# Cross-attention on one core: GpSimd's written order, the last batch's stages, transposes for the attention

## The chip, the core and the metric

The kernel runs on one core of one Trainium2 chip. The core has five instruction queues that matter here: TensorE (PE in the profile; PEld is its weight loads), VectorE (DVE), ScalarE (ACT), GpSimd (POOL) and SyncE (SP, which issues the transfers). Each queue is worked off in its own order; semaphores order the queues among each other. The metric is the device time of one execution in microseconds (us). The kernel before took 420.76 us (median of 3 runs, 420.61 to 422.99).

## What is computed

Cross-attention over 8 batches, 112 queries, 371 text tokens and 4 prompt tokens, 20 heads of 16 channels. Cut to what matters:

```python
q   = heads(x @ W_q)                                   # B 8, S 112, C 320, H 20, Dh 16
k_t, v_t = heads(text @ W_k), heads(text @ W_v)        # text: first 371 of 375 tokens, E 512
probs_t  = softmax(q k_t * Dh**-0.5)
text_out = probs_t @ v_t
k_ip, v_ip = heads(ip @ W_k_ip), heads(ip @ W_v_ip)    # ip: the last 4 tokens
qsem  = l2norm(probs_t @ text)                         # per head: 112 x 512
fused = q k_ip * Dh**-0.5 + 0.5 * qsem @ l2norm(ip).T
probs_ip = softmax(fused) * spatial_mask[:, None]
out = (text_out + probs_ip @ v_ip) @ W_out + b_out + x
```

All of it is in float32. The kernel never forms qsem: the norm of probs @ text is the root of p G p, where G is the Gram matrix of the text tokens, so the kernel multiplies the probabilities with a matrix u that holds G (its lower blocks only, doubled off the diagonal), the products with the normalised prompts, a column of ones and the values.

## The kernel before

**Tiling.** Each batch has 5 groups of 4 heads. For a group, `scores` writes four score products (112 x 375) to PSUM banks, `probabilities` takes the negated row maximum on VectorE (line 757), the exponential on ScalarE (line 760) and a copy of the four prompt logits, `ipl` (line 762); `sent` stores the probabilities to the ring `xg` by a transfer, and `turned` transposes them in blocks on VectorE (line 778). `multiplied` (line 797) is the large product: 12 steps of four products in four row strips of TensorE, each step 32 tokens narrower than the last (392 to 40 columns), into four banks `ps_qd`. Each bank then holds p G for its head, and in its last 21 columns the four prompt products, the sum z and the 16 value sums. `value_sums` copies these 21 to `pvs` on ScalarE (line 810); `reduced` multiplies p G with p and sums on VectorE (line 843), into `ss`. In the last batch, and for two heads of the group before it, `shared` does that sum by a copy on ScalarE (line 828), a product on GpSimd (line 832) and a sum on ScalarE (line 836). `placed` puts the group's values into u on GpSimd (line 703).

**Beside it, one batch ahead,** run the keys (line 582), values (616), queries (381) and the Gram matrix (540) of the next batches, cut into pieces and spread over the groups by `between`.

**The end of a batch** is `finish`, a generator whose pieces are called from the loop by `run(("f", b), ...)`: z2 and the maximum rn = max(ss, z2) (lines 884 and 886), a root on ScalarE (901) between two table loads (Sqrt, then Exp), the division of the value sums by z on GpSimd (`divided`, 892), the fused prompt logits fu (908 to 914), their Exp (918), and the weights w (926). For batches 0 to 5 `prompt_sums_and_projection` weighs the prompt values on GpSimd (986 to 994), transposes the attention (`ps_a`, 999) and projects it (`ps_o`, 1011). For the last two batches the prompt values come by a product: w is transposed (`ps_wT`, 932), then attention and prompts are summed in one bank `ps_a` (946: a product with the identity; 949: a product with the prompt values `bd`). `bd` holds the prompt values of both batches by head; a memset (683) and two selects on GpSimd (686, in `own_channels`) clear what belongs to other heads. The last batch's first 16 heads go through `finish` (generator `first`), its last 4 through `last_heads` (`last`), with `projected_prompts` (`late`) multiplying their prompt values with W_out beforehand.

**What sets the order.** The kernel asks the framework to keep the written order on TensorE, SyncE and VectorE (and from the main loop on ScalarE). GpSimd's queue is ordered by the framework's scheduler until the last batch, and as written from there. So before the last batch a scheduler decides which of GpSimd's ready instructions comes first; afterwards the text does.

**Banks.** PSUM has three pools: four banks `qd`, two `sc` and two `mm` (`bank(name)` takes `mm`, `bank(name, spare=True)` takes `sc`). A product that gets a bank again waits until the last reader of its former tile is done. In the last batch the odd groups use `mm` and `sc` for `ps_qd`, and the scores of group five lie in `qd`.

**The last batch's loop** runs over its five groups g = 0 to 4 with the scores of group four made in group one (two at step 0, two at step 3) and those of group five in group two (steps 2 and 3). `sums` is the open generator of `shared`; `before` is the open `finish` of the seventh batch (b = 6), whose root stands between group one and two; `last_keys` and a piece of the queries lie there too.

## Time and profile before

| | |
|---|---|
| median of 3 runs (lowest to highest) | 420.76 us (420.61 to 422.99) |
| the profiled execution | 420.08 us |
| its span | 418.3 us |
| busy: TensorE, weight loads | 410.9 us, 321.4 us |
| busy: VectorE, ScalarE, GpSimd | 334.5 us, 216.3 us, 123.6 us |
| the large product, line 797 | 3840 records, 218.5 us |
| block transposes of the probabilities, line 778 | 79, 126.0 us |
| chain that ended last | TensorE 90%, VectorE 3%, GpSimd 2%, ScalarE 2%, transfers 2% |

The span is the time from the first to the last instruction or transfer of the profiled execution. A row of a timeline gives start, duration, engine, source line, operation, the tile written and the tiles read, a count and, in brackets, how long the engine stood idle before it and what ended that. Times of weight loads overlap those of products. A product in plain float32 shows as two records, a transpose as one.

### The profile page before, as it was taken

The numbers are of one execution on the slowest core, as the hardware profiler recorded it, in microseconds if no ns is written. First come the engines' busy times: TensorE is split into PE (matmuls) and PEld (weight loads), VectorE is DVE, ScalarE is ACT, GpSimd is POOL, SyncE is SP. The second block draws the span as 40 slices with busy tenths as digits, with TensorE's granted clock in tenths as the row PEclk, the third lists the DMA queues.
The fourth block names the chain that finished last, engine by engine and source line by source line (L and its number), as shares of the span: only waits on it lengthen the run. The fifth ranks groups of instructions, "written<-read, shape, count | busy, mean of one in ns | idle before, by whom it ended". The sixth has DMA issues, their size and how long they took to land.

```text
span 418.3 us, 14151 instructions
## 1 busy us (share of the span) xinstructions
PE 410.9 (98%) x5512; PEld 321.4 (77%) x5512; DVE 334.5 (80%) x724; ACT 216.3 (52%) x732; POOL 123.6 (30%) x308
## 2 busy tenths in 40 slices
PE   8999999999999999999999999999999999989996
PEld 8767777787778877788777877788678887677983
DVE  4037689988899889898898978899798977878774
ACT  2344334736365453746356353654538463765774
POOL 3611121112071114422062121712144120724540
PEclk9999999999999999999999999999999999999999
DMA  8777856557764455465554555554445355526201
GB/s 247 211 189 201 184 144 155 150 133 172 176 164 130 134 142 142 113 157 164 142 134 126 170 133 136 133 126 143 121 123 137 97 169 151 144 75 168 69 2 31
DMA packets 47578, 58.98 MB, mean 141 GB/s; under 512 B 10648, under 2 KB 41536, under 8 KB 47510
## 3 DMA queue, kind: packets, MB, share of 16 engines
q1 hardware_dynamic: 46878, 57.10, 51.8%
q10 hardware_dynamic: 632, 0.96, 0.8%
q8 instruction: 44, 0.72, 0.8%
q14 instruction: 24, 0.20, 0.2%
HBM read 16.79 MB, written 1.88 MB: 45 GB/s over the span
## 4 chain that ended last, share of the span: by engine, by line
PE 90%; DVE 3%; POOL 2%; ACT 2%; DMA 2%; issue 1%; SPq 0%; DVEq 0%; POOLq 0%
PE ps_qd L797 37%; PE ps_v L616 13%; PE ps_s L734 10%; PE ps_k L582 10%; PE ps_g L540 7%; PE ps_q L381 3%; PE ps_o L1011 3%; PE ps_g L496 1%; DMA xg<-p 1%; DVE nmx L757 1%; ACT p L760 1%; DVE xgT L778 1%; PE ps_w L472 1%; PE ps_o L966 1%; PE ps_k L598 1%; POOL wv L986 1%
## 5 line engine op out<-in xcount | busy, mean ns | idle before, releaser
L797 PE MATMUL ps_qd<-u,xgT 32*112 32x168 f32 (+11 forms) x3840 | 218.5, 351 | 0.0
L797 PEld LDWEIGHTS ps_qd<-u,xgT 32*112 32x112 f32 x3840 | 185.0, 172 | 27.2 <-issue 0.7
L778 DVE STREAM_TRANSPOSE xgT<-xg 128x512 f32<-128x512 f32 (+2 forms) x79 | 126.0, 1604 | 4.3 <-DMA xg<-p 3.9
L760 ACT ACTIVATE p<-ps_s,nmx 112x371 f32<-112x371 f32 x156 | 84.5, 579 | 86.5 <-DVE nmx L757 81.2
L757 DVE TENSOR_REDUCE nmx<-ps_s 112x1 f32<-112x371 f32 x160 | 78.4, 534 | 25.1 <-PE ps_s L734 24.1
L843 DVE CUSTOM_DVE_ANT_0 junk<-ps_qd,p 112x371 f32<-112x371 f32 x146 | 79.2, 543 | 20.3 <-ACT pvs L810 3.3
L703 POOL COPY u<-vr 128x64 f32<-128x64 f32 x120 | 26.7, 240 | 138.4 <-PE ps_qd L797 106.5
L734 PE MATMUL ps_s<-kT,qm 32*112 32x375 f32 (+1 forms) x320 | 65.8, 496 | 0.0
L616 PE MATMUL ps_v<-wv_sb,ctxT 128*128 128x384 f32 (+1 forms) x192 | 63.0, 477 | 0.0
L616 PEld LDWEIGHTS ps_v<-wv_sb,ctxT 128*128 128x128 f32 x192 | 35.7, 190 | 20.9
L582 PE MATMUL ps_k<-ctxT,wk_sb 128*128 128x371 f32 x136 | 46.9, 488 | 0.2 <-DVE ctxT L463 0.2
L734 PEld LDWEIGHTS ps_s<-kT,qm 32*112 32x112 f32 x320 | 25.6, 171 | 12.7 <-issue 10.8
L582 PEld LDWEIGHTS ps_k<-ctxT,wk_sb 128*128 128x128 f32 x136 | 24.4, 189 | 14.0 <-issue 0.5
L651 ACT COPY vr<-vext 32x240 f32<-32x240 f32 x84 | 32.7, 389 | 1.3
L623 ACT COPY vext<-ps_v 128x384 f32<-128x384 f32 (+1 forms) x24 | 11.2, 466 | 42.2 <-PE ps_v L616 42.2
L540 PE MATMUL ps_g<-ctxT 128*32 128x375 f32 (+11 forms) x672 | 30.4, 333 | 0.0
L540 PEld LDWEIGHTS ps_g<-ctxT 128*32 128x32 f32 x672 | 27.7, 110 | 2.0
L390 DVE TENSOR_SCALAR qm<-ps_q,emask 128x224 f32<-128x224 f32 (+1 forms) x25 | 9.0, 394 | 18.1 <-PE ps_q L381 18.0
L762 ACT COPY ipl<-ps_s 112x4 f32<-112x4 f32 x140 | 23.0, 165 | 0.0
L986 POOL TENSOR_TENSOR wv<-vip,w 112x1280 f32<-112x1280 f32 x6 | 14.8, 2468 | 22.2 <-DVE w L926 22.2
L512 ACT ACTIVATE ug<-ps_g 128x375 f32<-128x375 f32 (+2 forms) x24 | 8.3, 375 | 24.7 <-PE ps_g L540 12.5
L442 DVE STREAM_TRANSPOSE ctxT<-ct 128x512 f32<-128x512 f32 x18 | 20.0, 1113 | 0.0
(177 smaller groups left out, 344.2 us busy)
## 6 DMA issues: line engine op xcount, KB each, us to landing
xg<-p SPq DMA_DIRECT2D x156, 162.3 KB
u<-ug SPq DMA_DIRECT2D x124, 99.0 KB
ct<-in_ctx_dram SPq DMA_DIRECT2D x24, 176.0 KB
vip<-vipd SPq DMA_DIRECT2D x6, 560.0 KB
out_dram<-ob SPq DMA_DIRECT2D x8, 140.0 KB
ct<-in_ctx_dram SPq DMA_DIRECT2D x4, 256.0 KB
x_sb<-in_x_dram SPq DMA_DIRECT2D x7, 140.0 KB
xr_sb<-in_x_dram SPq DMA_DIRECT2D x28, 35.0 KB
```

The lines of the kernel that those rows point to most:

```text
L540: nc.tensor.matmul(ps[c][q * RG : (q + 1) * RG, j * RG - c * P : T - c * P], ctxT[:, e, j * RG : (j + 1) * RG], ctxT[:, e, j * RG : T], st ...
L582: nc.tensor.matmul(ps[:, :TT], wk_sb[:, e, i * P : (i + 1) * P], s["ctxT"][:, e, :TT], start=(e == 0), stop=(e == NE - 1),)
L616: nc.tensor.matmul(ps[:, :w], ctxT[:, e, c * P : (c + 1) * P], wv_sb[:, e, :w], start=(e == 0), stop=(e == NE - 1),)
L651: copy(s["vr"][a * RG : (a + 1) * RG, q::QN].rearrange("p c g d -> p c (g d)"), s["vext"][q * RG : (q + 1) * RG, :, a * w : (a + 1) * w],)
L703: nc.gpsimd.tensor_copy(v, dealt(b, c, s["vr"][:, c * QN : (c + 1) * QN, g, :]))
L734: nc.tensor.matmul(ps[:S, :w], qm[a * RG : (a + 1) * RG, i, r, j * S : (j + 1) * S], s["kT"][a * RG : (a + 1) * RG, i, :w], start=True, st ...
L757: nc.vector.tensor_reduce(nmx, ps[:S, :TT], AX.X, ALU.max, negate=True)
L760: nc.scalar.activation(s["p", g][:, a, :], ps[:S, :TT], AF.Exp, bias=nmx)
L762: nc.scalar.copy(s["ipl"][:, groups[g][a], :], ps[:S, TT:T])
L778: nc.vector.transpose(xT[:, j0:j1].rearrange("p j (k q) -> p q j k", q=QN), xg[:, :, j0 * RG : j1 * RG].rearrange("p q (j k) -> p q j k", ...
L797: nc.tensor.matmul(banks[a][:S, j * RG : UW], xT[a * RG : (a + 1) * RG, j, :S], region(b, c)[a * RG : (a + 1) * RG, q, j * RG - c * P :], ...
L843: nc.vector.tensor_tensor_reduce(out=junk, in0=ps[:S, :TT], in1=s["p", g][:, a, :], scale=1.0, scalar=0.0, op0=ALU.mult, op1=ALU.add, accu ...
```

## The change

1. From the seventh batch's third group on (three steps before the last batch, at `n == len(steps) - NG - 3`) GpSimd too runs in written order, instead of from the last batch on. Its queue changes: in the fifth group of that batch the prompt sums of batch six (986 to 994) come ahead of the copies of vr, and the selects on bd behind these and the next copies into u.
2. The prompt logits of the first batch (`prompt_logits`) move behind the pieces that `between` issues: on TensorE behind the key transposes and a query product, on ScalarE behind the copy of kT.
3. `probabilities` is split into `maxima` and `exponentials`. In the last batch, `finish` of the seventh starts ahead of the loop (z2, reciprocal, division, then the bias and a table load for Sqrt); its maximum, root and the load of Exp come in step 0 of group one, between the maxima and the exponentials of the two held heads. The ScalarE sums of `shared` are drained at step 0 of group one, at the start of group two, and at step 8 of groups three and four. fu comes at step 4 of group two, behind the maxima for group five, its Exp at step 8, w at step 8 of group three.
4. The tail: `value_sums` of the last group come behind the copy of wT and in the order 0, 3, 2, 1; the third value copy of group four comes ahead of the last sum; the Sqrt table is loaded earlier; `last_heads` takes reciprocal and quotient ahead of the last reduction, and its transpose later; the copies `bw` and of the last `aT` move from ScalarE to VectorE; the last batch's `ps_a` takes an `sc` bank.
5. The identity products of `ps_a` in the last two batches become transposes (`is_transpose=True`), and the warming product `warm` ahead of them goes.

```diff
-    def warm(ps, n):
-        for _ in range(n):
-            nc.tensor.matmul(ps[:, NC * P :], ident, ident, start=True, stop=True)
...
+    def maxima(b, g, a):
+        s = st[b]
+        nmx = small.tile([S, 1], F32, tag="nmx", name=f"nmx_{b}_{g}_{a}", bufs=4)
+        nc.vector.tensor_reduce(nmx, s["sc", g, a][:S, :TT], AX.X, ALU.max, negate=True)
+        s["mx", g, a] = nmx
...
     def probabilities(b, g, a, hold=False):
-        s = st[b]
-        ps = s.pop(("sc", g, a))
-        nmx = small.tile([S, 1], F32, tag="nmx", name=f"nmx_{b}_{g}_{a}", bufs=4)
-        nc.vector.tensor_reduce(nmx, ps[:S, :TT], AX.X, ALU.max, negate=True)
+        maxima(b, g, a)
+        exponentials(b, g, a)
+        if not hold:
+            sent(b, g, a)
...
 finish:
+        def divided():
+            nc.vector.reciprocal(zr, z)
+            eng.tensor_tensor(
+                ah, pvs[:, :, NIP + 1 :], zr.unsqueeze(2).to_broadcast([S, n, D]), ALU.mult
+            )
...
-            with_bias(b)
+            if bd is None:
+                with_bias(b)
         nc.vector.scalar_tensor_tensor(z2, z, EPS * EPS, z, ALU.mult, ALU.mult)
+        if bd is not None:
+            divided()
+            yield
+
         nc.vector.tensor_tensor(rn, s["ss"][:, part], z2, ALU.max)
-        if bd is not None:
-            nc.vector.reciprocal(zr, z)
-            divided()
-        yield
+        if bd is None:
+            yield
 
         nc.scalar.activation(rn, rn, AF.Sqrt)
         nc.scalar.preload_act_table(AF.Exp)
...
-            ps = bank(f"ps_a_{b}_{h0}")
-            if b == B - 2:
-                warm(ps, 1)
+            ps = bank(f"ps_a_{b}_{h0}", spare=n < H)
             for i in range(i0, i1):
                 o = ps[:, i * S : (i + 1) * S]
                 nc.tensor.matmul(
-                    o, attn[:, i * P : (i + 1) * P], ident[:S, :S], start=True, stop=False
+                    o,
+                    attn[:, i * P : (i + 1) * P],
+                    ident[:S, :S],
+                    start=True,
+                    stop=False,
+                    is_transpose=True,
                 )
...
 projected_prompts:
-        nc.scalar.copy(bw, ps[:k, :C])
+        nc.vector.tensor_copy(bw, ps[:k, :C])
...
 last_heads:
         nc.vector.scalar_tensor_tensor(z2, z, EPS * EPS, z, ALU.mult, ALU.mult)
-        yield
-
-        nc.vector.tensor_tensor(rn, s["ss"][:, part], z2, ALU.max)
         nc.vector.reciprocal(zr, z)
...
+        yield
+
+        nc.vector.tensor_tensor(rn, s["ss"][:, part], z2, ALU.max)
         nc.scalar.activation(rn, rn, AF.Sqrt)
         nc.scalar.preload_act_table(AF.Exp)
-        ps = ps_qd.tile([P, 512], F32, tag="qd", name=f"ps_a_{b}_{h0}")
-        nc.tensor.transpose(ps[:, :S], attn[:, FULL * P :], ident[:S, :S])
-        yield
-
         nc.vector.reciprocal(rn, rn)
...
+        ps = ps_qd.tile([P, 512], F32, tag="qd", name=f"ps_a_{b}_{h0}")
+        nc.tensor.transpose(ps[:, :S], attn[:, FULL * P :], ident[:S, :S])
         aT = work.tile([P, NC, S], F32, tag="aT", name=f"aT_{b}_{h0}")
-        nc.scalar.copy(aT[:, FULL, :], ps[:, :S])
+        nc.vector.tensor_copy(aT[:, FULL, :], ps[:, :S])
+        yield
+
...
 main loop:
+        if n == len(steps) - NG - 3:
+            ctx.enter_context(
+                tc.manual_schedule(
+                    engines=engines | {mybir.EngineType.Activation, mybir.EngineType.Pool}
+                )
+            )
...
-        if n == NG - 1:
-            run(("t", b), lambda: prompt_logits(b))
...
         between(b, g)
+        if n == NG - 1:
+            drain(prompt_logits(b))
...
 last batch:
+    run(before, lambda: finish(b - 1, bd=bd[:, 0]))
+    with_bias(b - 1)
+    nc.scalar.preload_act_table(AF.Sqrt)
...
             run(("q", b), None)
-            nc.scalar.preload_act_table(AF.Sqrt)
-            run(before, None, 3)
+            drain(sums)
         for j, _ in enumerate(multiplied(b, g)):
+            if g == 0 and j == 0:
+                drain(sums)
             if g == 0 and j in (0, 3):
                 for a in (2, 3) if j == 0 else (0, 1):
-                    coming(NG - 2, a, bank(f"ps_s_{b}_{NG - 2}_{a}", spare=a > 1))
-            if g == 0 and j in (2, 3):
-                if j == 2:
+                    scores(b, NG - 2, a, ps=bank(f"ps_s_{b}_{NG - 2}_{a}", spare=a > 1))
+                if j == 0:
+                    for a in (2, 3):
+                        maxima(b, NG - 2, a)
+                    run(before, None)
+                    for a in (2, 3):
+                        exponentials(b, NG - 2, a)
                     drain(turned(b, 1))
-                for a in (2, 3) if j == 2 else (0, 1):
-                    sent(b, NG - 2, a)
+                    for a in (2, 3):
+                        sent(b, NG - 2, a)
+                else:
+                    for a in (0, 1):
+                        probabilities(b, NG - 2, a)
...
-            if g == 1 and j == 4:
+            if (g, j) in ((1, QN), (1, 2 * QN), (2, 2 * QN)):
                 run(before, None)
-            if g == 3 and j == 8:
+            if g > 1 and j == 2 * QN:
                 drain(sums)
...
-            drain(ahead)
         if g == 0:
-            run(before, lambda: finish(b - 1, bd=bd[:, 0]))
             with_bias(b)
...
-            value_sums(b, g, 1, 3)
+            value_sums(b, g, 1)
             placed(b, g + 1, (NT - 1,))
             drain(sums)
-            value_sums(b, g, 3)
...
```

45 lines of the change are left out of this document (18 added, 27 removed).

## The prediction

> **What bounds the kernel now.** I read the busy times of the page first, then a table of stretches, then the waits of TensorE, and after that the timelines of the places where it waits.
>
> ```profile
> PE 410.9 (98%) x5512; PEld 321.4 (77%) x5512; DVE 334.5 (80%) x724; ACT 216.3 (52%) x732; POOL 123.6 (30%) x308
> ...
> 415.00:418.30 3.30, 0.00 (x0) 0.00 (x0) 0.28 (x1) 0.00 (x0) 0.00 (x0) 0.96 0.16 48
> ...
> PE ps_a L999 <- POOL attn L994: 1.7, 1, 1.7
> PE ps_q L381 <- ACT ipl L720: 0.4, 1, 0.4
> ```
>
> The first row says that TensorE bounds the kernel: it is busy 98% of the span, VectorE 80%, with little room. What can shorten it is time in which TensorE stands still, or the work after its last large product. Two open waits show after the first 30 us: 1.7 us for the attention of the sixth batch (ps_a, line 999) and 0.4 us for the copy of the prompt logits. More waits hide inside "busy", since matmul ends are modelled; they show as a stage that takes longer than its like. These are the second to fifth group of the last batch, by the products of line 797 alone (start and end of the stretch, its length, then TensorE's busy time):
>
> ```profile
> 385.04:390.95 5.91, 5.91 (x95) 4.53 (x97) 1.00 0.27 80
> 390.95:396.60 5.65, 5.65 (x105) 5.11 (x104) 1.00 0.44 122
> 396.60:401.30 4.70, 4.70 (x107) 4.10 (x105) 1.00 0.01 3
> 401.30:406.06 4.76, 4.76 (x99) 4.12 (x95) 1.00 0.01 2
> ...
> PEld ps_qd L797 <- ACT kT L605: 0.6, 1, 0.6
> PEld ps_qd L797 <- ACT ipl L762: 0.5, 2, 0.3
> ```
>
> The fourth and fifth groups hold nothing but their products and take 4.70 and 4.76 us. The second also carries four score products and takes 5.91. The third carries none and takes 5.65: 0.95 too long. The last row names the cause: its banks come free with the last copies of ipl, behind the exponentials of group five, whose scores lie in them. Group two waits 0.6 for the copy of kT.
>
> The profiled execution took 420.08 us, 1.8 more than its span of 418.3, and lies 0.68 under the median of 420.76. I sum on the span and add the difference to the median at the end. "Old clock" below means the times of this trace.
>
> **Part 1: GpSimd in written order.**
>
> ```profile
> 356.62 0.30 DVE L926 SCALAR_TENSOR_TENSOR w<-ex,sm_sb,rx 112x80 f32<-112x80 f32 x1
> ...
> 357.38 1.67 POOL L651 COPY vr<-vext 32x240 f32<-32x240 f32 x4 [4.88 <-DMA u<-ug]
> 359.13 2.08 POOL L686 TENSOR_SCALAR_AFFINE_SELECT bd<-bd 80x640 f32<-80x640 f32 x2
> 361.18 2.47 POOL L986 TENSOR_TENSOR wv<-vip,w 112x1280 f32<-112x1280 f32 x1
> 363.72 1.54 POOL L992 TENSOR_TENSOR wv<-wv 112x640 f32<-112x640 f32 x1
> 365.35 0.86 POOL L993 TENSOR_TENSOR attn<-attn,wv 112x320 f32<-112x320 f32 x1
> 366.28 0.86 POOL L994 TENSOR_TENSOR attn<-attn,wv 112x320 f32<-112x320 f32 x1
> 367.08 0.58 POOL L703 COPY u<-vr 128x64 f32<-128x64 f32 x3
> ...
> 362.77 2.76 PE L582 MATMUL ps_k<-ctxT,wk_sb 128*128 128x371 f32 x8
> 367.19 0.51 PE L999 MATMUL ps_a<-ident,attn 112*128 112x112 f32 x3 [1.66 <-POOL attn L994]
> ```
>
> The scheduler had put the four copies of vr (1.67) and the two selects on bd (2.08) ahead of the prompt sums (lines 986 to 994), although w, which these need, was ready at 356.62 + 0.30 = 356.92. In written order the sums go first: 356.95 + 2.47 + 1.54 + 0.86 + 0.86 and four gaps of some 0.06 give 362.9. TensorE gets to ps_a at 362.77 + 2.76 = 365.53, so the stall of 1.66 goes whole, with 2.6 us in hand. What is queued behind the sums comes later: vr ends at 364.6, the three copies of u for the next group (0.58) at 365.2, and TensorE wants these only after ps_a and the query products; the selects end at 367.5, and nothing needs bd before the last stage. The queue ahead loses nothing: GpSimd had waited 4.88 us there, and a small copy into kT moves into that gap. **Gain 1.66**; the bounds are 1.0 (if the query copies on VectorE are held up by a select that now runs beside them, which no row shows) and 1.7.
>
> **Part 2: the prompt logits** move behind the key transposes and the queries. Then the queries no longer wait 0.4 us for their bank; the logits take the one that the copy of kT releases, about when TensorE gets there. **Gain 0.35**, between 0 and 0.4; as TensorE stays the bound after it, it is kept.
>
> **Part 3: the last batch's stages.** From here all is 1.66 earlier; "new clock" is the old one less 1.66.
>
> ```profile
> 375.54 1.90 POOL L832 TENSOR_TENSOR shared<-shared,p 112x371 f32<-112x371 f32 x2 [2.33 <-ACT shared L828]
> 386.40 0.86 POOL L857 TENSOR_TENSOR xb<-x_sb,bias_sb 112x320 f32<-112x320 f32 x1
> ...
> 378.58 2.99 DVE L778 STREAM_TRANSPOSE xgT<-xg 128x768 f32<-128x768 f32 x2
> 385.86 0.62 DVE L886 TENSOR_TENSOR rn<-ss,z 112x20 f32<-112x20 f32 x1
> 389.35 1.89 DVE L757 TENSOR_REDUCE nmx<-ps_s 112x1 f32<-112x371 f32 x4
> 404.72 0.17 DVE L886 TENSOR_TENSOR rn<-ss,z 112x16 f32<-112x16 f32 x1
> ...
> 385.86 1.28 ACT L1374 ACT_TABLE_LOAD   x1
> 387.15 0.22 ACT L901 ACTIVATE rn<-rn 112x20 f32<-112x20 f32 x1
> 391.44 0.62 ACT L760 ACTIVATE p<-ps_s,nmx 112x371 f32<-112x371 f32 x1
> ...
> 387.25 0.56 PE L734 MATMUL ps_s<-kT,qm 32*112 32x375 f32 x1
> 388.12 0.58 PE L734 MATMUL ps_s<-kT,qm 32*112 32x375 f32 x3
> ```
>
> The seventh batch's root (maximum, Sqrt, two table loads) moves from 385.86 into the first group. VectorE there waits at the maximum for two sums of ScalarE, and these for GpSimd's products (375.54 + 1.90, so 375.8 on the new clock); the sums end at about 376.6. Then comes a price that the rows show: this maximum took 0.62 at 385.86, where one like it took 0.17 at 404.72, and it ended as a GpSimd product of shared did. Now GpSimd runs attn and xb there (0.86 the second), so I let the maximum end at 377.8, 0.8 late. Behind it on VectorE stand the transposes for group two (2.99, to 380.8; needed at 385.04 - 1.66 = 383.4), two score maxima (half of 1.89), a reduction, the next transposes (another 3.0, to 385.2) and the query copy, to 385.4; the scores that need it come at 387.25 - 1.66 = 385.6. So the chain holds with 0.2 us to spare. On ScalarE, Sqrt ends at 378.0, the load (1.28) at 379.3, and the first held exponential at 380.0, just as TensorE wants its bank for the last keys. The copy of kT comes as late in group two as before: two sums left the queue ahead of it, but the exponentials there come later by about as much. **Group two: 0**, between -0.5 and +0.3.
>
> The load costs nothing beyond its 1.28: the Sqrt starts 0.01 after it. The Trainium skill, "ScalarE: Activation LUTs", section "What ACT_TABLE_LOAD costs", adds a drain of about 1.38 us to each switch; by that rule the two loads now ahead of the held exponentials would delay the last keys by an estimated 1.6 us and take that from the sum. The trace speaks against it.
>
> Group three: the four maxima for group five (389.35) stood on VectorE behind the chain of fu, which had waited for the Sqrt. Now they come first. The last score ends at 388.12 + 0.58 = 388.7 on the old clock, its maximum half a us later, its exponential and ipl at about 390.2 instead of 392.06, and group three can start at 390.95 unhindered; fu and its Exp follow while VectorE would wait for products anyway. **Gain 0.9**, between 0.5 and 0.95. What is late next are the transposes for groups four and five, by this count 1.0 and 0.2 us ahead of their use.
>
> **Part 4: the tail.**
>
> ```profile
> 402.24 0.47 ACT L828 COPY shared<-ps_qd 112x371 f32<-112x371 f32 x1
> 410.70 0.21 ACT L1073 ACTIVATE rn_last<-rn_last 112x4 f32<-112x4 f32 x1
> ...
> 404.49 0.19 DVE L884 SCALAR_TENSOR_TENSOR z<-pvs 112x16 f32<-112x16 f32 x1 [1.08 <-ACT pvs L810]
> 410.38 0.16 DVE L1064 TENSOR_TENSOR rn_last<-ss,z_last 112x4 f32<-112x4 f32 x1
> 410.67 0.23 DVE L1067 TENSOR_TENSOR attn<-pvs,zr_last 112x64 f32<-112x64 f32 x1
> ...
> 413.18 0.26 PE L1098 MATMUL ps_wT<-ident,w_last 112*16 112x112 f32 x1
> 413.91 0.79 PE L1106 MATMUL ps_o<-bw,wT_last 16*112 16x320 f32 x2
> ...
> 406.57 0.42 PE ps_a L477 x2
> 406.99 0.21 PE ps_a L946 x2
> ```
>
> ScalarE's sums of group three now end before group four does (401.30), so the copy for GpSimd at 402.24 comes about 0.8 earlier, and pvs, for which VectorE waited 1.08, stands ahead of the sum. The maximum at 404.72 comes 0.85 earlier, and with it the whole chain to the last four reductions. From that go 0.4: the last heads' reciprocal and quotient, which lay between 410.54 and 410.90, now stand ahead of the last reduction. The last maximum starts at 409.9 instead of 410.38, and its Sqrt, which then waits for no copy of aT on ScalarE, at 410.1 instead of 410.70. The copies of aT and bw, now on VectorE ahead of the last sums, cost 0 to 0.4 of that. The last transposes come at 412.6 instead of 413.18; what follows (the last product to 413.91 + 0.79 = 414.7, the addition, the store) is the same. **Gain 0.6**, between 0 and 1.3.
>
> This holds the transposes too. A plain product with the identity is two records (0.21), a transpose one (three for three at 367.19), so five records of 0.1 and the warming product (0.42) leave TensorE, 0.9 in all. But TensorE then waits that much longer for the last weights, so by itself this is worth 0 to 0.3, and the 0.6 has it.
>
> Sum: 1.66 + 0.35 + 0 + 0.9 + 0.6 = 3.5 us. Span 414.8, execution 416.6, and 0.68 to the median: **417.2**.
>
> **Rivals.** (a) *More waits go*: 0.3 of group two's wait as well, and the tail, bound by TensorE, gains 1.2. Then 1.7 + 0.4 + 0.3 + 0.95 + 1.2 = 4.5: 416.2. For it: each is a wait that a row shows. Against: VectorE's chain binds the tail as I count it.
> (b) *VectorE's queue behind the root becomes the bound.* Its spare is 0.2 us at the query copy; TensorE pays every later end of the root than 378.0 one for one at the scores of group two. If GpSimd's attn and xb together stand ahead of the maximum, or the held exponentials delay the keys, that is 1.5 to 2.5: 418.7 to 419.7. For it: VectorE's 80%. Against: GpSimd is idle 70% of the span.
> (c) *The clock falls in the tail*, slower than before. It is 1.00 by each stretch of the last batch and 0.96 in the last row, when TensorE has stopped. If it halved once the warming product is gone and transposes stand in for products, between half and all of TensorE's 8.6 us from 406.06 to 414.7 would come on top: 421.5 to 425.8. It decides if it falls before about 409. Against: the transposes at 367.19 came behind a stall and the products after them ran at 1.00. The Trainium skill, "TensorE: Matmul & The Clock Gate", section "Part 4: PE-mode transpose", says that transposes do not count as busy for the gate; by that rule a drop is possible, but products stand between them here.
> (d) *GpSimd's order isn't the cause* of the stall at 367.19: something else ends there. Then 1.8 remains: 418.9. Against: the row names line 994, which is last in GpSimd's chain.
>
> **How the numbers follow.** Forecast 0.54, (a) 0.17, (b) 0.17, (c) 0.05, (d) 0.07. One per cent is 4.2 us, about what a measurement of this kernel can tell from no change; faster means under 416.55. The forecast is 0.65 above this and unsure by about 1 us: of it 0.10 falls below, with (a) 0.27. Slower means over 424.97: the upper end of (c) and what (b) leaves open, 0.05. The rest, 0.68, is within 1%. Range: from (a) with the bounds of its terms, 415.3, to the upper end of (b), 419.8.
>
> **What would show it.** Right: ps_a of the sixth batch starts without a wait; group three of the last batch takes about 4.7 us of products; the seventh batch's Sqrt lies beside group one; the last transposes come 6.5 us after the end of group five instead of 7.1. Wrong: a new wait of TensorE at the last keys or at the scores of group two, VectorE standing longer at the root's maximum, or a clock under 1.00 before the last addition.

## The result

| | before | after |
|---|---|---|
| median of 13 runs each (lowest to highest) | 420.84 us (420.08 to 422.99) | 417.67 us (416.23 to 419.64) |
| ratio to before, 95% interval | 1 | 0.9917 (0.9899 to 0.9934) |
| the profiled execution, its span | 420.08 us, 418.3 us | 419.28 us, 417.6 us |

The time fell by 0.83%, with an interval of 0.66 to 1.01%: 3.5 us of 420.84. The forecast was 417.2 with 415.3 to 419.8.

### The profile after

The busy line of the page:

```profile
PE 410.9 (98%) x5505; PEld 322.8 (77%) x5505; DVE 333.9 (80%) x726; ACT 217.0 (52%) x730; POOL 123.3 (30%) x308
```

It is the line of before almost to the digit, and the two profiled spans differ by 0.7 us only. Whoever stops here finds the change without effect. But the two traces are not level when they reach the code that was changed. This is the key product with which the last batch's group one nears its end (line 582 before, 577 after), and it begins at 362.77 in the trace of before:

```profile
365.74 2.76 PE L577 MATMUL ps_k<-ctxT,wk_sb 128*128 128x371 f32 x8
```

The changed kernel's profiled execution is 2.97 us late by then, and only part 2 and the beginning of part 1 have run. Of the 2.97, 2.63 are there at the last scores within the first batch's fifth group (80.26 before, 82.89 after), ahead of everything that was moved. VectorE's waits in the first 80 us, which both programs spend alike, show transfers that land later in the one trace; first the trace of before, then that of after (total, times, longest):

```profile
DVE xgT L778 <- DMA xg<-p: 2.9, 3, 1.4
DVE xgT L778 <- DMA ct<-in_ctx_dram: 0.4, 1, 0.4
```

```profile
DVE xgT L781 <- DMA xg<-p: 4.0, 3, 1.8
DVE xgT L781 <- DMA ct<-in_ctx_dram: 1.6, 1, 1.6
```

In these two rows that is 2.3 us more of waits for transfers. The executions of either kernel spread over 3 us, and the one that was profiled after is among its longer ones (419.28, median 417.67). So I compare the traces from the start of that key product on. From there traces of the same code agree to a few hundredths: up to the last keys it is 17.04 in the changed kernel and 17.03 to 17.05 in ten variants of it.

| from the key product's start | before | after | gain |
|---|---|---|---|
| to the end of group five (first ps_wT) | 43.29 | 39.94 | 3.35 |
| from there to the last addition (ob) | 8.73 | 8.36 | 0.37 |
| to the end of the span | 55.52 | 51.82 | 3.70 |

TensorE's waits after the first 30 us:

```profile
PE ps_wT L1104 <- DVE w_last L1099: 0.7, 1, 0.7
PE ps_ip L708 <- ACT kT L573: 0.5, 1, 0.5
```

The wait of 1.7 for the attention is gone; the 0.4 for the prompt logits has become 0.5 for the copy of kT; and a wait of 0.7 stands in the tail that was not there before. GpSimd's queue and TensorE around the sixth batch's attention:

```profile
359.96 2.46 POOL L992 TENSOR_TENSOR wv<-vip,w 112x1280 f32<-112x1280 f32 x1 [4.34 <-DVE w L929]
...
365.06 0.86 POOL L1000 TENSOR_TENSOR attn<-attn,wv 112x320 f32<-112x320 f32 x1
365.86 1.64 POOL L646 COPY vr<-vext 32x240 f32<-32x240 f32 x4
```

```profile
368.33 0.45 PE L1005 MATMUL ps_a<-ident,attn 112*128 112x112 f32 x3
```

The sums go first and are done 2.4 us before ps_a, which waits for nothing. It follows the key product's start by 2.59 instead of 4.42. That is 1.83 less, 0.17 more than the wait's row showed: a product's modelled end (365.74 + 2.76 = 368.50) lies behind the start of the next, so the idle time in such a row is too short by that overlap.

The second and third group of the last batch, by the large products alone (length, then TensorE's busy time):

```profile
386.13:391.55 5.42, 5.42 (x99) 4.33 (x102) 1.00 0.30 89
391.55:396.25 4.70, 4.70 (x100) 4.41 (x98) 1.00 0.53 147
```

Before they took 5.91 and 5.65. Group three has the forecast 4.7; group two is 0.49 shorter, which was not forecast.

### The profile page after: what moved, and what is told of

It is laid out like the page before. It is cut to its first block, busy times and chain, and to the rows that moved or that the text cites. A ratio compares the mean times of both kernels' runs of the same rounds, so it can differ in the third digit from the quotient of the medians.

```text
span 417.6 us, 14139 instructions
## 1 busy us (share of the span) xinstructions
PE 410.9 (98%) x5505; PEld 322.8 (77%) x5505; DVE 333.9 (80%) x726; ACT 217.0 (52%) x730; POOL 123.3 (30%) x308
## 4 chain that ended last, share of the span: by engine, by line
PE 90%; DMA 3%; DVE 2%; ACT 2%; issue 1%; SPq 1%; POOL 0%; DVEq 0%; ACTq 0%; POOLq 0%
PE ps_qd L800 38%; PE ps_v L611 15%; PE ps_s L729 10%; PE ps_k L577 10%; PE ps_g L535 7%; DMA xg<-p 3%; PE ps_o L1017 3%; PE ps_q L381 2%; PE ps_g L491 1%; PE ps_w L472 1%; DVE nmx L751 1%; PE ps_k L593 1%; PE ps_c L455 1%; ACT p L765 0%; DVE xgT L781 0%
```

## The experiments

Each ratio is to the kernel before on the same chip, with its 95% interval. The intervals are 1.5 to 3 us wide, so they tell a variant from the kernel before but not from each other; the stretches of the traces do that (us from the key product's start). The expectations took the end from spans given to 0.1 us, so their figures differ from the last column by up to 0.05. The rows "part 1 alone" and "part 3 alone" are the kernel before with that part; those below are the changed kernel with something altered.

| kernel | ratio (interval) | to the end of group five | from there to the last addition | to the end |
|---|---|---|---|---|
| before | 1 | 43.29 | 8.73 | 55.52 |
| changed | 0.9917 (0.9899 to 0.9934) | 39.94 | 8.36 | 51.82 |
| part 1 alone | 0.9959 (0.9935 to 0.9983) | 41.42 | 8.81 | 53.70 |
| part 3 alone | 0.9944 (0.9918 to 0.9969) | 41.82 | 8.52 | 53.84 |
| without parts 4, 5 | 0.9919 (0.9890 to 0.9947) | 39.92 | 8.51 | 51.88 |
| without part 5 | 0.9928 (0.9902 to 0.9954) | 39.93 | 8.79 | 52.23 |
| without part 4 | 0.9885 (0.9849 to 0.9922) | 39.94 | 8.01 | 51.45 |
| without part 2 | 0.9905 (0.9872 to 0.9937) | 39.95 | 8.58 | 51.94 |
| logits in the group | 0.9894 (0.9861 to 0.9928) | 39.94 | 8.57 | 52.01 |
| early x | 0.9920 (0.9888 to 0.9953) | 40.49 | 8.58 | 52.57 |
| sum ahead of the copy | 0.9911 (0.9879 to 0.9944) | 39.94 | 8.35 | 51.78 |
| combo | 0.9902 (0.9867 to 0.9937) | 39.93 | 8.01 | 51.39 |
| combo, early load | 0.9912 (0.9887 to 0.9937) | 39.93 | 9.71 | 53.13 |
| the same with products | 0.9919 (0.9890 to 0.9948) | 39.92 | 8.98 | 52.33 |

### Part 1 alone, part 3 alone

The kernel before with GpSimd's written order:

```diff
     for n, (b, g) in enumerate(steps[:-NG]):
+        if n == len(steps) - NG - 3:
+            ctx.enter_context(
+                tc.manual_schedule(
+                    engines=engines | {mybir.EngineType.Activation, mybir.EngineType.Pool}
+                )
+            )
...
-    ctx.enter_context(
-        tc.manual_schedule(
-            engines=engines | {mybir.EngineType.Activation, mybir.EngineType.Pool}
-        )
-    )
```

> The kernel before with part 1 of the change alone: GpSimd in written order from the seventh batch's third group. Theory (GpSimd's order made the stall ahead of ps_a of the sixth batch): TensorE's wait of 1.66 us there goes, nothing takes its place, and the stretch from the start of the last batch's second key product (line 582 of the kernel before, at 362.77) to the end of the span falls from 55.5 to about 53.7 us; the ratio to the kernel before is about 0.996. Rival (the wait only moves on, to the copies of vr and u that now come later): the stretch stays at 55.0 to 55.5 and the ratio at 1.000.

And the kernel before with the stages of the last batch alone, whose core is:

```diff
-                    coming(NG - 2, a, bank(f"ps_s_{b}_{NG - 2}_{a}", spare=a > 1))
+                    scores(b, NG - 2, a, ps=bank(f"ps_s_{b}_{NG - 2}_{a}", spare=a > 1))
+                if j == 0:
+                    for a in (2, 3):
+                        maxima(b, NG - 2, a)
+                    run(before, None)
+                    for a in (2, 3):
+                        exponentials(b, NG - 2, a)
...
-            if g == 1 and j == 4:
+            if (g, j) in ((1, QN), (1, 2 * QN), (2, 2 * QN)):
                 run(before, None)
```

> The kernel before with part 3 alone: the seventh batch's root and table loads in group one of the last batch, sums drained earlier, maxima for group five ahead of fu; GpSimd's order, the logits, the tail and the products with the identity as before. Theory: groups two and three lose their waits, 0.5 and 0.95, and the sums of group three end earlier, so that the stretch from the second key product to the end is about 53.7 instead of 55.5, while the 1.66 us wait at ps_a stays; ratio 0.996. Rival (VectorE's wait at the root eats it, as it has no 1.66 us in hand here): a new wait at the last keys or at the scores of group two, and a stretch of 54.7 or more.

ps_a of the sixth batch, first with the order alone, then with the stages alone:

```profile
366.24 0.45 PE L999 MATMUL ps_a<-ident,attn 112*128 112x112 f32 x3
```

```profile
368.08 0.51 PE L1007 MATMUL ps_a<-ident,attn 112*128 112x112 f32 x3 [1.67 <-POOL attn L1002]
```

Up to the end of group five the order alone takes the wait away and with it 1.87 (43.29 to 41.42); the stages alone leave the wait where it was and take 1.47. Together they make 3.34 of the 3.35: two independent gains, which add up. The stages alone also take 0.21 of the tail (8.73 to 8.52). Rival (d) falls.

### Without the tail's order, without the transposes, and without the order but with the transposes

Three kernels take parts 4 and 5 off the changed one: both; part 5 (plain products and the warming product again); part 4 (the old tail, with transposes). Part 5 undone:

```diff
+            if b == B - 2:
+                warm(ps, 1)
...
-                    is_transpose=True,
```

Part 4 undone, cut to its core:

```diff
-            value_sums(b, g, 1)
+            value_sums(b, g, 1, 3)
             placed(b, g + 1, (NT - 1,))
             drain(sums)
+            value_sums(b, g, 3)
...
-    nc.scalar.preload_act_table(AF.Sqrt)
+    value_sums(b, g)
     next(first)
...
-    for a in (0, 3, 2, 1):
-        value_sums(b, g, a, a + 1)
...
+    nc.scalar.preload_act_table(AF.Sqrt)
+    reduced(b, g, 2, 3)
```

> The changed kernel with parts 4 and 5 undone: the tail's order of before, identity products and the warming product. Theory (the tail is bound by the chain over VectorE and ScalarE, and its reorder is worth little): the stretch from the second key product to the end grows from 51.9 to 52.3, ratio to the kernel before 0.9925. Rival (the tail carries the gain that the earlier sums bring, and without it that is lost): 52.9 or more.

> The changed kernel with part 5 alone undone: five plain products with the identity, and the warming product ahead of them. Theory (TensorE waits 0.68 us for the last weights anyway, so its 0.95 us less is mostly hidden): that wait shrinks to near nothing and the stretch from the second key product to the end grows by 0.1 to 0.35, from 51.9 to at most 52.2. Rival (TensorE binds the tail): it grows by 0.95, to 52.8. The granted clock stays at 1.00 in both up to the last addition.

> The changed kernel with part 4 undone (the old tail) but with the transposes of part 5 and no warming product. With both parts undone the stretch from the second key product of the last batch to the end took 51.87, as in the changed kernel (51.86); with part 5 alone undone 52.24. If part 4 itself costs 0.4 and part 5 gains 0.4, the stretch here is 51.3 to 51.6: TensorE reaches the last weights' transpose up to 0.9 earlier, the copy of wT, the Sqrt load and the Sqrt behind it on ScalarE come about 0.5 earlier, and VectorE's last weights end the tail. If instead the transposes only gain what part 4's order gives them room for, VectorE's weights bind here as they did with both undone, and the stretch stays at 51.8 to 51.9 with a wait of TensorE of 0.5 or more for w_last.

Up to the end of the span the four kernels form a square: 51.88 with neither part 4 nor part 5, 52.23 with part 4 alone, 51.45 with part 5 alone, 51.82 with both. Part 5 gains 0.43 on the old tail and 0.41 on the new one, and part 4 costs 0.37 with transposes and 0.35 without. Together they are worth 0.06 (0.15 up to the last addition, 8.51 to 8.36); I had expected 0.4. More than half of the tail's 0.37 comes from part 3, whose sums of group four are done earlier.

Why the transposes gain on the old tail, where the prediction let TensorE only wait longer for the last weights: the last heads' Sqrt there stands behind a load and a copy that wait for TensorE. ScalarE and TensorE of that kernel (old tail, transposes):

```profile
407.37 0.24 ACT L941 COPY wT<-ps_wT 64x112 f32<-64x112 f32 x1
407.63 1.28 ACT L1444 ACT_TABLE_LOAD   x1
...
409.17 0.21 ACT L1079 ACTIVATE rn_last<-rn_last 112x4 f32<-112x4 f32 x1
```

```profile
411.65 0.26 PE L1104 MATMUL ps_wT<-ident,w_last 112*16 112x112 f32 x1 [0.32 <-DVE w_last L1099]
```

When TensorE gets to the second ps_wT sooner, the copy, the load and the Sqrt follow, and so the last weights: the Sqrt starts 3.92 behind the first ps_wT here and 4.43 behind it with plain products. Why part 4 costs shows in the changed kernel's trace, ScalarE and then VectorE:

```profile
406.40 1.28 ACT L1436 ACT_TABLE_LOAD   x1
407.70 0.25 ACT L941 COPY wT<-ps_wT 64x112 f32<-64x112 f32 x1
407.85 0.39 ACT L813 COPY pvs<-ps_qd 112x21 f32<-112x21 f32 x4
```

```profile
408.19 0.54 DVE L846 CUSTOM_DVE_ANT_0 junk<-ps_qd,p 112x371 f32<-112x371 f32 x1 [0.41 <-ACT pvs L813]
```

The last group's value copies now stand behind the load, and VectorE's third reduction waits 0.41 for them; reciprocal and quotient (408.74 to 409.18) come on top ahead of the fourth. The last maximum starts 3.99 behind the first ps_wT instead of 3.38, and its Sqrt, which no longer stands behind a copy, 4.19 instead of 3.92.

### The sum ahead of the value copy

The three kernels with part 4 that ran after these had a tail of 8.57 or 8.58, not 8.36, with the same code. Their VectorE and GpSimd differ from the changed kernel at one place, the maximum of the first 16 heads. First the changed kernel, then the one without part 2:

```profile
403.77 0.17 DVE L901 TENSOR_TENSOR rn<-ss,z 112x16 f32<-112x16 f32 x1
403.76 0.67 POOL L888 TENSOR_TENSOR attn<-pvs,zr 112x256 f32<-112x256 f32 x1 [1.13 <-ACT shared L839]
```

```profile
402.78 0.66 DVE L901 TENSOR_TENSOR rn<-ss,z 112x16 f32<-112x16 f32 x1
402.77 0.63 POOL L888 TENSOR_TENSOR attn<-pvs,zr 112x256 f32<-112x256 f32 x1 [1.13 <-ACT shared L839]
```

The two instructions start within 0.01 us of each other. In one execution the maximum takes 0.17 and GpSimd is 0.04 longer than in the other, in which the maximum ends with GpSimd. It is a race, and it arises because part 4 puts the value copy ahead of the last sum of ScalarE: the maximum waits for the sum, and so does not start before the division. I put that copy back:

```diff
-            value_sums(b, g, 1)
+            value_sums(b, g, 1, 3)
             placed(b, g + 1, (NT - 1,))
             drain(sums)
+            value_sums(b, g, 3)
```

> The changed kernel with one piece of part 4 undone: the third value copy of group four stands behind the last ScalarE sum again, as before. In the changed kernel's order this sum ends as GpSimd starts the division of the first 16 heads, and the maximum rn (line 901) and that division start within 0.01 us of each other: rn took 0.17 in the changed kernel's trace (403.77) and in the one without transposes, but 0.65 to 0.66 in the three others with this order, where it ended with the division. If the piece makes this race, rn takes 0.13 to 0.17 here, starts right behind the reciprocal zr and some 0.2 ahead of the division, and Sqrt starts 1.85 to 1.9 ahead of the last batch's first ps_wT instead of 1.70 (changed kernel) or 1.22 (lost race). The stretch from that ps_wT to the last addition, 8.36 in the changed kernel and 8.57 where the race was lost, is then 8.3 to 8.4, bound by the value copies of the last group behind the Sqrt load. Rival: the maximum is held up here too (0.6 or more), so the order of sum and copy isn't what makes it, and the stretch is 8.5 to 8.6.

The maximum took 0.13 and GpSimd's division began 0.23 after it; Sqrt started 1.89 ahead of the first ps_wT, the stretch was 8.35. So the race goes with the piece. In five profiled executions with the piece it was lost three times, at 0.2 us each in the tail.

### Part 2 undone, and the prompt logits in the group

Undone:

```diff
+        if n == NG - 1:
+            run(("t", b), lambda: prompt_logits(b))
...
-        if n == NG - 1:
-            drain(prompt_logits(b))
```

In the loop over the group's steps:

```diff
+            if n == NG - 1 and j == 8:
+                drain(prompt_logits(b))
...
-        if n == NG - 1:
-            drain(prompt_logits(b))
```

> The changed kernel with part 2 undone: the prompt logits of the first batch stand ahead of the pieces again. Measured from the end of the first batch's last group on TensorE to the scores behind the pieces: 2.85 us before, 2.90 us after, because the wait of 0.4 for the bank behind the logits became a wait of 0.5 for the copy of kT. If part 2 is worth nothing, this stretch takes 2.8 to 2.9 us here with a wait for ipl (line 720) and none for kT, and the whole time is the changed kernel's. If part 2 gained the predicted 0.35 and its trace only fell badly, the stretch takes 3.2 us or more.

> The changed kernel with the prompt logits issued at step 8 of the first batch's last group, among the large products: their copy on ScalarE then has a third of the group to finish, ahead of the queries. If what part 2 lacked is only time between the logits and the next user of their bank, both waits go: no wait for ipl and none for kT at the end of the first batch, and the stretch of logits, key transposes and queries is 0.4 to 0.5 shorter than the changed kernel's 2.90 (to 2.4, of which the logits' 0.7 now lie in the group). Rival: the logits in the group wait for their bank themselves, or the query products then wait for the copies of the group's exponentials; then TensorE loses as much there.

From the last scores within the first batch's fifth group to those behind the pieces it is 84.91 - 80.26 = 4.65 in the trace of before, 87.59 - 82.89 = 4.70 in the changed kernel, 4.70 without part 2. In the changed kernel TensorE, the copy of kT on ScalarE, and the transposes on VectorE ahead of the exponentials:

```profile
82.89 0.48 PE L729 MATMUL ps_s<-kT,qm 32*112 32x375 f32 x2
...
84.69 0.54 PE L568 MATMUL ps_k<-ident,k 128*128 128x128 f32 x3
...
86.89 0.76 PE L708 MATMUL ps_ip<-kipb,qT 128*112 128x32 f32 x6 [0.52 <-ACT kT L573]
87.59 0.57 PE L729 MATMUL ps_s<-kT,qm 32*112 32x375 f32 x2
```

```profile
86.30 0.54 ACT L573 COPY kT<-ps_k 128x371 f32<-128x371 f32 x1
```

```profile
82.60 2.05 DVE L781 STREAM_TRANSPOSE xgT<-xg 128x1024 f32<-128x1024 f32 x1 [0.32 <-DMA xg<-p]
```

The logits wait for the bank that the key transposes (84.69) fill and the copy of kT empties, and that copy stands on ScalarE behind two exponentials and the value copies until 86.30. In this execution the exponentials are late themselves, since VectorE had waited 0.32 for a transfer. With the logits among the large products:

```profile
82.11 0.76 PE L708 MATMUL ps_ip<-kipb,qT 128*112 128x32 f32 x6
...
85.18 0.57 PE L729 MATMUL ps_s<-kT,qm 32*112 32x375 f32 x2
```

No wait of TensorE is left at this place, and the stretch is 85.18 - 80.84 = 4.34: 0.36 shorter. It is not kept. Counted from the last scores within the fifth group, the traces fall into these sets (us; "next scores" are those after the ones behind the pieces):

| kernels | scores behind the pieces | VectorE's first reduction | next scores | key product of the last batch |
|---|---|---|---|---|
| logits ahead of the pieces: before, part 1 alone, part 3 alone | 4.64 to 4.65 | 2.92 to 2.94 | 8.21 to 8.24 | 282.39 to 282.51 |
| the same: without part 2 | 4.70 | 2.99 | 8.28 | 282.46 |
| part 2: without parts 4, 5; without part 5; sum ahead of the copy | 4.24 to 4.26 | 2.93 to 2.95 | 8.22 to 8.23 | 282.41 to 282.42 |
| part 2: changed; without part 4; early x | 4.67 to 4.78 | 3.35 to 3.46 | 8.64 to 8.75 | 282.83 to 282.94 |
| logits in the group, combo and its two variants | 4.32 to 4.34 | 3.05 to 3.07 | 8.33 to 8.36 | 282.52 to 282.54 |

In three of the six traces with part 2 TensorE does not stand still for kT and gains 0.4 at the scores behind the pieces, as forecast; in the three others VectorE's transposes waited 0.3 to 0.4 for a transfer (xg). But the next scores come 5.27 to 5.30 behind VectorE's first reduction in every one of the 14 traces, whatever TensorE gained before. The weight loads of the next large products wait for those reductions in the kernel with the logits in the group (the trace of before shows no such wait):

```profile
PEld ps_qd L800 <- DVE ss L846: 0.9, 2, 0.4
```

So VectorE's queue bounds this place, part 2 is worth nothing, and the logits in the group are worth nothing either: what TensorE saves it waits out in the next group, and the distance to the key product stays that of before.

### x loaded earlier

In the changed kernel the root's maximum took 0.17, not the 0.8 more that I had priced, and GpSimd's addition xb was not beside it. VectorE, then GpSimd:

```profile
377.75 0.83 DVE L896 SCALAR_TENSOR_TENSOR z<-pvs 112x20 f32<-112x20 f32 x1
...
379.67 0.17 DVE L901 TENSOR_TENSOR rn<-ss,z 112x20 f32<-112x20 f32 x1
```

```profile
376.64 1.90 POOL L835 TENSOR_TENSOR shared<-shared,p 112x371 f32<-112x371 f32 x2 [2.34 <-ACT shared L831]
...
383.32 0.86 POOL L860 TENSOR_TENSOR xb<-x_sb,bias_sb 112x320 f32<-112x320 f32 x1 [3.72 <-DMA x_sb<-in_x_dram]
```

z did pay such a price (0.83, ending at 378.58 as the products of shared end at 378.54); the maximum did not, because xb waited 3.72 for the transfer of x. So I issued that transfer a group earlier:

```diff
-        if g == NG - 1:
-            load_x(b, b + 1 if b < B - 2 else B)
+        if g == NG - 1 and b < B - 2:
+            load_x(b, b + 1)
+        elif b == B - 2 and g == NG - 2:
+            load_x(b, B)
```

> The changed kernel with the transfer of x for the last two batches issued one group earlier, so that GpSimd's addition xb no longer waits for it (it started 3.7 us after the division, at 383.32, with the releaser DMA) and runs right behind the division, beside the root's maximum. The prediction had priced that maximum at 0.8 more, because a VectorE operation of two SBUF operands ends only as the GpSimd operation beside it does. If that price is right and was only avoided by the late transfer, the maximum rn takes 0.6 to 0.9 here instead of 0.17, ends with xb, and Sqrt, load and the held exponentials come 0.6 to 0.8 later; the last keys then wait 0.3 to 0.5 for their bank, and the stretch from the second key product of the last batch to the end is that much longer than 51.9. If the price is wrong, rn takes 0.17 with xb beside it and the stretch is unchanged. A third way: rn stretches, and the spare of about 1.9 us that VectorE has behind it takes it up; then rn takes 0.6 to 0.9 and the stretch stays 51.9.

```profile
379.23 0.80 DVE L901 TENSOR_TENSOR rn<-ss,z 112x20 f32<-112x20 f32 x1
```

```profile
379.12 0.86 POOL L860 TENSOR_TENSOR xb<-x_sb,bias_sb 112x320 f32<-112x320 f32 x1
```

```profile
PEld ps_qd L800 <- ACT ipl L767: 0.3, 1, 0.3
PEld ps_qd L800 <- ACT kT L600: 0.2, 1, 0.2
```

The maximum takes 0.80 and ends with xb. The last keys do not wait (17.05 from the key product, as before), so the place that I expected was wrong; but the held exponentials come 0.6 later and with them the copies of kT and ipl, and TensorE's weight loads wait 0.2 and 0.3 in groups two and three, where the changed kernel shows no such wait. The stretch to the end of group five grows by 0.55 (39.94 to 40.49). An earlier transfer makes this kernel slower there.

### The old tail with the logits in the group, and an earlier load

The old tail with transposes, and the logits in the group; then the same with the load for Sqrt moved ahead of the copies of wT and aT:

```diff
     value_sums(b, g)
+    nc.scalar.preload_act_table(AF.Sqrt)
     next(first)
...
-    nc.scalar.preload_act_table(AF.Sqrt)
     reduced(b, g, 2, 3)
```

> Both things that helped together: old tail with transposes and no warming product, and the prompt logits of the first batch in its last group. From the parts: stretch at the end of the first batch 0.36 shorter than the changed kernel's (4.34 from the scores in the last group to those behind it, instead of 4.70), stretch from the second key product of the last batch to the end 51.5 instead of 51.9 to 52.0. Together some 0.8 us under the changed kernel: 416.5 to 417.2 if the kernel before takes 420.8 in this call, ratio 0.989 to 0.991. Rival: the 0.36 is given back later, in a wait for a transfer that then lands no earlier; the time is then the changed kernel's less 0.4.

> The kernel called combo with the last table load for Sqrt ahead of the copies of wT and aT, behind the value copies of the last group. With the old tail and transposes the Sqrt of the last heads started at 409.17, 0.38 after its maximum was done (408.63 + 0.16), because the load (407.63) stood behind two copies that wait for TensorE. Loaded from about 406.3 on, it delays the second copy of wT by at most 0.2, and Sqrt starts 0.2 to 0.4 earlier: the wait of TensorE for w_last (0.32) goes, and the stretch from the first ps_wT to the last addition is 7.7 to 7.85 instead of 8.01. Rival: the load delays the copies of wT and aT, TensorE waits for these instead (0.1 to 0.4 at ps_a or ps_o), and the stretch stays 8.0 or grows.

The first kept the tail's gain: 51.39 from the key product on, 0.43 less than the changed kernel. At the first batch it took 4.32 (84.76 - 80.44), but the rival came true for these 0.4: they are given back by the next scores, as the table above shows. Its median is 417.19 us, its ratio 0.9902: below the kernel before for certain, below the changed kernel by less than the intervals can show.

The second went wrong in a way that neither expectation had. TensorE, and then the stretches of its trace (length, busy time of the five engines, granted clock, share of the transfers):

```profile
406.94 0.32 PE L947 MATMUL ps_a<-ident,attn 112*128 112x112 f32 x1 [0.41 <-ACT wT L941]
407.08 0.74 PE L955 MATMUL ps_a<-wT,bd 80*128 80x112 f32 x2
...
408.22 2.90 PE L972 MATMUL ps_o<-wo_sb,aT 128*112 128x320 f32 x6
```

```profile
406.00:408.00 2.00, 1.58 (x7) 1.09 (x6) 1.71 (x10) 0.92 (x3) 0.00 (x0) 0.76 0.05 12
408.00:410.00 2.00, 2.00 (x7) 1.33 (x6) 0.86 (x5) 1.46 (x3) 0.00 (x0) 0.50 0.00 0
```

The load holds up the copy of wT, as the rival said, and TensorE waits 0.41. But then the granted clock falls to half, and the six products of ps_o take 2.90 instead of 1.78. In stretches of half a microsecond the clock is 1.00 up to 407.0, 0.56 in the next, 0.53 in the one that ends at 410.5 and 1.00 behind it: some 3.4 us at 0.50. It is what rival (c) feared, seen in one profiled execution of a neighbour of the changed kernel. The last run asked whether the wait is enough, or transposes must stand ahead of it:

```diff
-                    is_transpose=True,
...
-    value_sums(b, g)
+    for _ in range(3):
+        value_sums(b, g)
     nc.scalar.preload_act_table(AF.Sqrt)
```

> The kernel called best with plain products with the identity in place of the transposes of the last two batches, and with the four value copies of the last group made three times, so that the copy of wT behind the Sqrt load again comes later than TensorE wants it. In best TensorE waited 0.41 for that copy at 406.5 and its granted clock then was 0.50 from 407.05 to 410.25: the six products of ps_o took 2.90 instead of 1.78, and the stretch from the first ps_wT to the last addition 9.71. Two or three of its 12 executions show such a mean clock (0.996 to 0.997). If a wait there is enough for the clock to fall, whatever ran before it, some executions here show a mean clock of 0.996 as well, and a profile that catches one shows 0.50 behind the wait. If transposes ahead of the wait are needed, the clock stays 1.00 in all of them, with a wait of 0.3 to 0.7 for wT, and the stretch is 8.3 to 8.9. With an event in a sixth of the executions, its absence in six here would not settle it; its presence would.

```profile
406.00:408.00 2.00, 1.27 (x8) 0.53 (x8) 1.71 (x8) 1.86 (x3) 0.00 (x0) 1.00 0.00 0
408.00:410.00 2.00, 2.00 (x13) 1.63 (x14) 1.22 (x8) 0.94 (x3) 0.00 (x0) 1.00 0.05 12
```

Behind plain products TensorE waited longer (0.72, for wT) and its clock stayed 1.00, in a stretch of 8.98, somewhat over the 8.3 to 8.9 expected; the mean clock of its six executions is 0.998 to 1.000. That fits transposes as a condition, and as the expectation says it does not settle it. Nor can the mean clock count the event, as I had meant to: the time behind TensorE's last product is in it (logits in the group has 0.996 as its mean and 1.00 in every stretch from 360 to that product, at 411), and the kernel before has executions at 0.995 to 0.997. So in how many executions of the early load the clock fell, and what made it fall, stays open.

## Why the prediction was right

The likeliest case came out: 417.67 where 417.2 was forecast, no change by 1%. Its sum of 3.5 is also what the ratio gives. That the sum fits so well is in part luck: one term of it is worth nothing, the tail gave less, and two others gave more. By its steps:

- **Part 1, right.** Forecast 1.66, measured 1.83 at ps_a and 1.87 alone. The size was off by the overlap of modelled ends, and above the upper bound of 1.7. Nothing that was queued behind the sums (vr, u, the selects) made anyone wait. The lower bound's reason, a query copy held up by a select, did not occur.
- **Part 2, wrong.** Forecast 0.35, measured nothing. The step that failed is "as TensorE stays the bound after it, it is kept". TensorE isn't the bound there: VectorE's reductions are, and a wait of TensorE that goes comes back in the next group as one for them. The step ahead of it, that the logits get their bank "about when TensorE gets there", held in three traces and not in the three in which VectorE had waited for a transfer; I had no row for when the copy of kT ends.
- **Part 3, group three, right:** 0.95 for 0.9.
- **Part 3, group two, wrong by 0.5.** The price at the root's maximum is real (0.80 beside xb when x is there), and I let it be paid because "now GpSimd runs attn and xb there". I had not asked when the data of xb land: the addition waited 3.72 for its transfer, the maximum went free, and the wait for the copy of kT went. That copy came 19.84 behind the key product, 20.33 with the price paid (early x) and 20.64 with the order alone. So 0.5 of these 0.8 come from the free maximum, and 0.3 would have come with the price too, where I had said "as late in group two as before". The early x shows it from the other side: with the price paid, 0.2 of the kT wait and 0.3 of the ipl wait are back. Of the 1.44 that groups two and three gained (5.91 and 5.65 to 5.42 and 4.70), 0.55 go, and 0.89 are left, which is the forecast.
- **Tail, some 0.6 of the forecast.** Forecast 0.6, measured 0.37 to the last addition, and 0.15 where the race is lost. The last transposes came 6.75 after the end of group five, not 6.5. Three terms lie in it, by the stretch to the last addition: part 3's earlier sums 0.21 (8.73 to 8.52 with the stages alone), part 5 0.43 on the new tail (8.79 to 8.36; forecast 0 to 0.3), part 4 -0.28 (8.51 to 8.79; forecast as the gain). The step that failed is that the copies cost "0 to 0.4" and the rest gains: I did not follow the value copies, which the diff puts behind the load of 1.28.
- **Errors that cancelled:** -0.35 in part 2 and -0.2 in the tail against +0.2 in part 1 and +0.5 in group two. The lower end of the range does not follow from its terms: the upper bounds 1.7, 0.4, 0.3, 0.95 and 1.3 make 4.65, or 416.1, where 415.3 was stated.
- **The rivals.** (a) was half right (group two's wait went, the tail did not become TensorE's). (b) has its mechanism, as the early x shows, but 0.55 over groups two and three is all it cost there; VectorE's queue does bound the place of part 2, where (b) did not look. (d) fell. (c) did not happen in the changed kernel, whose clock is 1.00 in every stretch of the last batch up to TensorE's last product, but the clock did fall in a neighbour of it, for 3.4 us. There the tail took 9.71 instead of 8.01; 0.4 of these 1.7 are the wait, and 1.1 the six products alone. By the Trainium skill, "TensorE: Matmul & The Clock Gate", section "Part 4: PE-mode transpose", a transpose does not count as busy in the way that a product does; the two last runs fit that and do not prove it, and seven other kernels with transposes kept 1.00 up to TensorE's last product.
- **The table loads.** On ScalarE, the root's load of Exp and the first held exponential behind it:

```profile
380.11 1.28 ACT L906 ACT_TABLE_LOAD   x1
381.40 0.57 ACT L765 ACTIVATE wv_sb<-ps_s,nmx 112x371 f32<-112x371 f32 x1
```

The exponential starts 0.01 after the load's end. The Trainium skill, "ScalarE: Activation LUTs", section "What ACT_TABLE_LOAD costs", adds a drain of about 1.38 us to each switch; this trace shows none, and the last keys came on time.

## What to carry to other kernels

A wait that goes from one row is a gain only if the landmark behind the next wait comes earlier too: the 0.4 at the prompt logits came back one group later, in another engine's name. Before pricing a contention or crediting a removed wait, find the time at which the other side is ready: the end of a copy in its own queue, the landing of a transfer; the name in the wait's row only says who was last this time. When two profiled spans differ by less than the runs of one kernel do, compare stretches from a landmark just ahead of the change, and look for code that both share but that runs differently. Where one engine's instruction and another's become ready at the same moment and share a resource, put a fixed order between them: otherwise the time is drawn by lot in each execution.

## What the runs showed of the hardware

- The elementwise VectorE operations on two operands in SBUF that are shown here wait out a GpSimd product that is ahead of them: the maximum takes 0.13 to 0.17 alone or ahead of it, and 0.65 to 0.80 when GpSimd is first, and ends with it. Who is first was decided within 0.01 us. VectorE's block transposes beside three GpSimd products of shared (2.72 in all) took 3.05 for two, and 2.98 without them.
- The granted clock fell to 0.50 for about 3.4 us, 0.1 us after TensorE took up work again behind a wait of 0.41 in the tail of one trace, and nowhere else ahead of TensorE's last product in the last batch of any trace here; a wait of 1.66 behind the key product, before the change, left it at 1.00.
- Programs that share all their code up to there reach the last scores of the first batch's fifth group at 80.26 to 82.89 from trace to trace, with later transfers in VectorE's waits; in the last 50 us traces of the same code agree to 0.1, but for the race.
